# Rounding passes of a feed-forward's weights paired beside a group's sums, and keys and queries set two slots apart

## The chip, the cores and the metric

The kernel runs on one core of a Trainium2 chip. The metric is the device time of one launch in microseconds; the number given is the median of several runs. TensorE, VectorE (DVE), ScalarE (ACT), GpSimd (POOL) and SyncE (SP) each work through a queue of their own, in its order; an instruction that needs another engine's result, or a buffer that another engine still reads, waits at the head of its queue, and all that stands behind it waits too.

## What is computed

Two layers over `x` of shape (4, 512, 256), each a cross-attention on a context and a feed-forward, both behind a layernorm and a gate. Attention has 16 heads of width 16. Shortened from the reference:

```python
x = x + tanh(g_xattn[0]) * L0_xattn(layernorm(x), ctx, ctx)   # scores + time bias, softmax
x = x + tanh(g_ffn[0]) * L0_ffn(layernorm(x))
x = x + tanh(g_xattn[1]) * L1_xattn(layernorm(x), ctx, ctx)
x = x + tanh(g_ffn[1]) * L1_ffn(layernorm(x))                 # routed to one of four experts
```

The first feed-forward uses ternary weights. This is what the rounding passes compute:

```python
def _quantize(W):
    gamma = jnp.mean(jnp.abs(W))
    return jnp.clip(jnp.round(W / (gamma + EPS)), -1.0, 1.0)
h = relu(einsum('bsd,fd->bsf', x, _quantize(W1)) + b1)
out = einsum('bsf,df->bsd', h, _quantize(W2)) + b2
```

Rounding and clipping together mean +1 where a weight is above half of (gamma + EPS), -1 where it is below minus that half, and 0 between.

## The kernel before

**Groups and slots.** Attention is cut into groups of four heads: two layers, four batch elements and four groups each make 32 groups, and each group has four *slots*, one for each 128 positions of the keys. The loop over `u` (L1250) walks 128 such slots. In each, `scores` (L498) puts on TensorE four products of 512 columns for the maxima of a slot six ahead (`pm`) and four for the softmax weights of this slot (`psc`). VectorE reduces each `pm` to a maximum (L512), ScalarE turns each `psc` into exponentials (L527), and in layer 0 GpSimd multiplies a 128 x 256 part of these by a decay (L530, called a *map* below). The eight products take the eight PSUM banks in turn, so the next product on TensorE needs the bank of the slot's first `pm`, which its maximum has to empty.

**Fixed jobs of a slot.** Every fourth slot (`u % 4 == 0`) starts with `weighted` (L555), the *sums* of the group just finished: 16 matmuls of 512 columns, which the trace shows as 32 rows. Where `u % 4 == 2`, `shifted` (L569, L571) and, in the first batch element and in layer 1, `divided` (L606 to L616) follow. For the other batch elements of layer 0 `divided_blocks` (L586 to L596) stands in slots with `u % 4 == 0`.

**The planner.** All other work lies in chains: lists of steps with a cost for TensorE and a gap in slots to the step before. `chain(steps, start, end, *after)` counts due slots back from `end`. In each slot the planner (`slot`) takes, among the chains that are ready, the step that is due first, as long as the slot's cost stays within `SLOT` = 3.1 or the step has no cost or is due. The order in which jobs are called is the order in each engine's queue; no other scheduler moves anything on TensorE, VectorE, ScalarE and GpSimd.

**The steps that the change touches.** `quantize` returns, for each of the two weights (`w1` and `w2`, each 128 x 2048 numbers in place): `totals`, two halves of the sum of absolute values on ScalarE; `total` (L283) and `limits` (L287 on TensorE, L290 to L292 on VectorE), which make the two thresholds `thr`; then for each of four parts of 512 columns `under(i)` (L299), a GpSimd pass that marks what is below the lower threshold, and `over(i)` (L306), a VectorE pass that reads the weights and that mark, and writes the rounded weights. In before these eight passes form one chain with at least one slot between neighbours, `under(i)` ahead of `over(i-1)`; `w1`'s chain starts in slot 4, `w2`'s in slot 17, behind it.

`project(layer, b, tt)` gives two steps: `keys` (a product at L455, then two VectorE passes at L465 in layer 0) and `queries` (a product at L455, then, for layer 0 and the first two batch elements, two ScalarE passes at L485). For the second batch element of layer 0 they stand, both in one slot, in slots 5 and 13.

Around them: `output_bias` (L265 to L269) in slot 6; the layernorm statistics of the third batch element (L329, L330) in slots 18 and 19, with its small GpSimd steps (`more_stats`, L334 to L347) in slot 19 and its rows on ScalarE (L360) in slot 20; `output_biases` of the first feed-forward (L631, a GpSimd pass over 128 x 1024) in slot 19; two `product` steps with the weight `wo` (L383, L388) in slots 21 and 22. `w1` is first read in slot 27 (L668), `w2` in slot 35.

The slots of the passes in before, and of keys and queries of the second batch element:

| step | slots before |
|---|---|
| `limits` of w1; w2 | 6; 18 |
| `under(0..3)` of w1 | 7, 8, 10, 12 |
| `over(0..3)` of w1 | 9, 11, 13, 15 |
| `under(0..3)` of w2 | 19, 20, 22, 24 |
| `over(0..3)` of w2 | 21, 23, 25, 27 |
| keys and queries, first half of the heads | 5, 5 |
| keys and queries, second half | 13, 13 |

Of the kernel before, what the change touches and what calls it, by code (L numbers as in the profile page):

```python
# [41 lines left out]
LEAD = 6  # L42
# [9 lines left out]
def flamingo_kernel(ctx: ExitStack, tc: tile.TileContext, t: dict, out: bass.AP):  # L52
# [11 lines left out]
    def bank_psum(name):  # L64
        return ps.tile([P, 512], F32, tag="bank", name=name)
# [43 lines left out]
    def weight_place(name):  # L109
        return wts.tile([P, NC * FF + NF], F32, tag="wff", name=name)  # L110

    w1f, w2f = (weight_place(name)[:, 0 : NC * FF] for name in ("w1q", "w2q"))
# [159 lines left out]
    def quantize(flat, name):  # L272

        thr = sml.tile([P, 2], F32, tag="qthr", name=f"qthr_{name}")
        part = sml.tile([P, 4], F32, tag="qpart", name=f"qpart_{name}")

        def totals(i0):
            for i in (i0, i0 + 1):
                dump = wts.tile([P, 512], F32, tag="h", name=f"abs_{name}{i}", bufs=8)
                nc.scalar.activation(dump, flat[:, ts(i, 512)], AF.Abs, accum_out=part[:, i : i + 1])  # L280

        def total():
            nc.vector.tensor_reduce(part[:, 0:1], part, AX.X, ALU.add)  # L283

        def limits():
            tot = bank_psum(f"qtot_{name}")
            nc.tensor.matmul(tot[:, 0:1], lhsT=ones, rhs=part[:, 0:1], start=True, stop=True)  # L287

            mean = sml.tile([P, 1], F32, tag="qmean", name=f"qmean_{name}")
            nc.vector.tensor_scalar(mean, tot[:, 0:1], 1.0 / (D * FF), 1e-5, ALU.mult, ALU.add)  # L290
            nc.vector.tensor_scalar(thr[:, 0:1], mean, 0.5, None, ALU.mult)
            nc.vector.tensor_scalar(thr[:, 1:2], mean, -0.5, None, ALU.mult)  # L292

        negs = {}

        def under(i):
            def run():
                negs[i] = wts.tile([P, 512], F32, tag="h", name=f"neg_{name}{i}", bufs=8)
                nc.gpsimd.tensor_scalar(negs[i], flat[:, ts(i, 512)], thr[:, 1:2], None, ALU.is_lt)  # L299

            return run

        def over(i):
            def run():
                w = flat[:, ts(i, 512)]
                nc.vector.scalar_tensor_tensor(w, w, thr[:, 0:1], negs[i], ALU.is_gt, ALU.subtract)  # L306

            return run

        return [  # L310
            (totals, 0, 0), (total, 0, 1), (limits, 0.2, 1),
            (under(0), 0, 1), *((f, 0, 1) for i in range(1, 4) for f in (under(i), over(i - 1))),
            (over(3), 0, 2),
        ]


    def layernorm(src, dst, eps, name, eng=None, meanwhile=None):
# [130 lines left out]
    def project(layer, b, tt):  # L448

        nm = f"{layer}_{b}{tt}"  # L450

        def product(w, src, name):
            pp = bank_psum(f"{name}{nm}")
            for c in range(NC):
                nc.tensor.matmul(  # L455
                    pp, lhsT=attn_w[layer][w][:, c, ts(tt, P)], rhs=src[:, c, :],
                    start=(c == 0), stop=(c == NC - 1),
                )
            return pp

        def key_half(pk, e):
            k = act.tile([P, S], F32, tag="k", name=f"k{nm}{e}", bufs=5)
            h = half[:, e : e + 1]
            if layer == 0:
                nc.vector.scalar_tensor_tensor(k, pk, h, kext[tt, e], ALU.mult, ALU.add)  # L465
            elif e == 0:
                nc.scalar.activation(k, pk, AF.Relu, bias=kone[:, e : e + 1], scale=h)
            else:
                nc.vector.tensor_scalar(k, pk, h, kone[:, e : e + 1], ALU.mult, ALU.max)
            ks[layer, b, tt, e] = k  # L470

        def keys(between=None, halves=range(2)):
            pk = product("wk", cT[b], "pk")
            if between:
                between()
            for e in halves:
                key_half(pk, e)

        def queries():
            pq = product("wq", xTs[layer, b], "pq")  # L480
            for e in range(2):
                q = act.tile([P, S], F32, tag="q", name=f"q{nm}{e}", bufs=4)
                h = half[:, e : e + 1]
                if layer == 0 and (e == 0 or b < 2):
                    nc.scalar.activation(q, pq, AF.Identity, bias=bqk[:, 0, tt, e : e + 1], scale=h)  # L485
                elif layer == 0:
                    nc.vector.tensor_scalar(q, pq, h, bqk[:, 0, tt, e : e + 1], ALU.mult, ALU.add)
                elif e == 0:
                    nc.scalar.activation(q, pq, AF.Relu, scale=h)
                else:  # L490
                    nc.vector.tensor_scalar(q, pq, h, 0.0, ALU.mult, ALU.max)
                qs[layer, b, tt, e] = q

        return [(keys, 1.75, 1), (queries, 1.75, 0)]
# [633 lines left out]
    def chain(steps, start, end, *after):  # L1128
        last = [end] * len(steps)
        for i in range(len(steps) - 2, -1, -1):  # L1130
            last[i] = last[i + 1] - max(steps[i + 1][2], 1 if steps[i][1] and steps[i + 1][1] else 0)
        c = dict(steps=list(zip(steps, last)), ready=start, after=after, done=None)
        chains.append(c)
        return c

    def first_unit(layer, b):
        return 4 * NT * (B * layer + b)
# [3 lines left out]
    for b in range(B):  # L1141
        first, rest = ffn0(b)
# [4 lines left out]
    for layer in range(2):  # L1147
        for b in range(B):
            u0 = first_unit(layer, b)
            lead, values = prepare(layer, b)  # L1150
            if (layer, b) == (0, 1):
                *early, early_rows, turn_1 = (job for job, *_ in lead)
                (early_values, *_), later_values = values
                turned_1 = chain([later_values, (turn_1, 0.9, 1)], 1, 4)
                chain(project(layer, b, 0), 5, u0 - LEAD - 2, turned_1)
            elif u0:
                chain(
                    [*lead, *project(layer, b, 0)], u0 - 14, u0 - LEAD - 2,
                    ffns[b] if layer else None,
                )  # L1160
                chain(values, u0 - 8, u0 + 2)
            chain(project(layer, b, 1), max(u0 - 4, 0), u0)
    (totals1, *_), *quant1 = quantize(w1f, "w1")
    (totals2, *_), *quant2 = quantize(w2f, "w2")
    totals = {0: (totals1, 0), 1: (totals1, 2), 2: (totals2, 0), 3: (totals2, 2)}
    quant = chain(quant1, 4, 17)
    chain(quant2, 17, 33, quant)
    chain([(bias_columns, 0, 0), (output_bias, 0.9, 2)], 4, 14)
    def step(f, *args, cost=0, gap=0):
        return (lambda: f(*args), cost, gap)  # L1170
# [7 lines left out]
    for b in range(B - 1):  # L1178
        u0 = first_unit(1, b + 1)
# [70 lines left out]
    for u in range(-NT, n_units):  # L1250
# [22 lines left out]
        if u in totals:  # L1273
            job, i = totals[u]
# [83 lines left out]
    first = LISTS[2][1]  # L1358
# [131 lines left out]
```

## Time and profile before

| what | value |
|---|---|
| median of three runs | 844.43 us (844.37 to 845.02) |
| the profiled execution's own time | 841.69 us |
| its span, first to last instruction | 839.6 us |
| granted TensorE clock, mean | 0.993 |
| slots 5 to 16, start of slot 5 to start of slot 17 on TensorE | 54.32 to 107.24 us |
| sums in slots 8, 12, 16 on TensorE | from 69.41 to 72.98, 85.4 to 88.96, 103.67 to 107.24 us |
| DMA queues, largest share of the span | 9.3% |

A row of instructions in order of time gives the start (us from the span's start), the length from the first start to the last end, engine, line, operation, what is written and read, shapes, how many followed each other, and in brackets how long the engine was idle ahead of it and what ended that. A row of groups gives, behind the bar, the busy time, the mean of one in ns, and the idle time ahead with its releasers. `PEld` is TensorE's weight load, which runs beside matmuls and shows best when TensorE had to wait. The engines' shares of busy time are means over stages with different limits, so what a slot costs has to be read from that slot.

### The profile page before, as it was taken

Reading aid. Unit: us, or ns where it says so; the run is one execution under the profiler, and the core shown is the slowest. Engines: PE = TensorE matmul, PEld = TensorE weight load, DVE = VectorE, ACT = ScalarE, POOL = GpSimd, SP = SyncE. Lnnn points to the kernel's source line nnn. Section 1 sums busy time; section 2 is a strip of 40 time slices with the busy share of each in tenths; the row PEclk is TensorE's granted clock in tenths of the full one; section 3 lists DMA queues with packets and bytes.
Section 4 is the critical chain, followed back from the end, with each engine's and each line's share of the span. In section 5 each row is a group of like instructions: output and inputs, shape, how many; then the busy total and the mean of one; then the engine's idle time right before and its main releaser. Section 6 shows DMA issues by size and latency. Waiting matters only on the chain. (4 is left out here: it accounts for less than half of the span.)

```text
span 839.6 us, 13573 instructions
## 1 busy us (share of the span) xinstructions
PE 809.5 (96%) x5220; PEld 452.3 (54%) x5220; DVE 568.7 (68%) x1272; ACT 422.1 (50%) x884; POOL 270.3 (32%) x439
## 2 busy tenths in 40 slices
PE   6999999999999999999999999999999999997995
PEld 3444344535464345544474444554445546896994
DVE  6868868766857676567746777448688663886443
ACT  2575555653645453455526475336655667332341
POOL 5636445524233253321101030002103422544522
PEclk9999999999999999999999999999999999998998
DMA  9200000000001000000000000000104331736620
GB/s 313 72 1 1 1 1 1 1 1 1 1 1 39 1 1 1 1 27 1 1 1 26 1 24 28 1 1 1 52 1 152 126 106 59 284 119 218 241 78 31
DMA packets 17712, 42.27 MB, mean 50 GB/s; under 512 B 2033, under 2 KB 12017, under 8 KB 15217
## 3 DMA queue, kind: packets, MB, share of 16 engines
q0 software_dynamic: 5104, 27.34, 9.3%
q1 hardware_dynamic: 12128, 13.54, 4.8%
q8 instruction: 41, 0.67, 0.3%
q10 hardware_dynamic: 416, 0.54, 0.2%
q14 instruction: 23, 0.18, 0.1%
HBM read 35.13 MB, written 6.29 MB: 49 GB/s over the span
## 5 line engine op out<-in xcount | busy, mean ns | idle before, releaser
L512 DVE TENSOR_REDUCE m<-pm 128x1 f32<-128x512 f32 x512 | 316.8, 682 | 107.2 <-PE psc L498 104.8
L527 ACT ACTIVATE p<-psc 128x512 f32<-128x512 f32 x512 | 267.1, 602 | 151.4 <-PE psc L498 148.9
L498 PE MATMUL psc<-q,k 32*128 32x512 f32 x1024 | 278.3, 622 | 0.2 <-DVE h L676 0.2
L498 PE MATMUL pm<-k,q 32*128 32x512 f32 x1024 | 262.2, 615 | 1.5 <-ACT q L485 0.9
L530 POOL TENSOR_TENSOR p<-p,dec 128x256 f32<-128x256 f32 x128 | 93.6, 735 | 177.1 <-ACT p L527 177.1
L498 PEld LDWEIGHTS pm<-k,q 32*128 32x128 f32 x1024 | 92.7, 184 | 83.8 <-issue 49.8
L498 PEld LDWEIGHTS psc<-q,k 32*128 32x128 f32 x1024 | 106.2, 183 | 51.6 <-issue 25.5
L555 PE MATMUL po<-p,v 128*32 128x512 f32 x1024 | 116.5, 595 | 1.9 <-DVE m L512 1.9
L555 PEld LDWEIGHTS po<-p,v 128*32 128x32 f32 x1024 | 31.7, 109 | 81.8 <-issue 60.8
L1090 PE MATMUL pg<-xs,wg 128*128 128x128 f32 x608 | 71.6, 276 | 0.4 <-DVE m L512 0.4
L1090 PEld LDWEIGHTS pg<-xs,wg 128*128 128x128 f32 x608 | 69.8, 192 | 3.8 <-DVE m L512 1.4
L623 POOL TENSOR_TENSOR x<-x,o 128x256 f32<-128x256 f32 x14 | 10.2, 728 | 174.4 <-DVE o L616 131.7
L1116 ACT ACTIVATE ha<-pg,wg 128x128 f32<-128x128 f32 x120 | 34.2, 368 | 53.6 <-PE pg L1090 53.6
L668 PE MATMUL ph<-xTf,w1q 128*128 128x512 f32 x128 | 60.0, 605 | 0.0
L1285 PE MATMUL pyf<-wo,ha 128*128 128x256 f32 x256 | 58.6, 384 | 0.0
L561 ACT COPY oT<-po 128x512 f32<-128x512 f32 x32 | 18.7, 584 | 77.1 <-PE po L555 77.1
L383 PE MATMUL py_f<-w2q,h 128*128 128x256 f32 x256 | 57.2, 381 | 0.0
L383 PEld LDWEIGHTS py_f<-w2q,h 128*128 128x128 f32 x256 | 48.0, 190 | 9.4 <-DVE m L512 3.0
L1285 PEld LDWEIGHTS pyf<-wo,ha 128*128 128x128 f32 x256 | 48.4, 194 | 6.2
L455 PE MATMUL pk<-cT,wk 128*128 128x512 f32 x68 | 35.3, 644 | 7.2 <-DMA cT<-in_ctxT_dram 7.2
L668 PEld LDWEIGHTS ph<-xTf,w1q 128*128 128x128 f32 x128 | 22.6, 189 | 30.4 <-issue 18.2
L388 DVE SCALAR_TENSOR_TENSOR x<-py_f,tg,x 128x512 f32<-128x512 f32 x8 | 6.0, 751 | 42.8 <-PE py_f L383 42.8
(256 smaller groups left out, 814.6 us busy)
## 6 DMA issues: line engine op xcount, KB each, us to landing
x<-in_x_dram SPq DMA_DIRECT2D x4, 512.0 KB, 8.8
rows_d<-xn_f SPq DMA_DIRECT2D x4, 512.0 KB, 3.0
rows_d<-x SPq DMA_DIRECT2D x4, 512.0 KB, 3.6
cT<-in_ctxT_dram SPq DMA_DIRECT2D x3, 512.0 KB, 9.6
w1q<-in_w_dram SPq DMA_DIRECT2D x1, 1024.0 KB, 8.9
w2q<-in_w_dram SPq DMA_DIRECT2D x1, 1024.0 KB, 11.2
wo<-in_wo_dram SPq DMA_DIRECT2D x2, 512.0 KB, 3.8
rows<-in_rows_dram SPq DMA_DIRECT2D x1, 640.0 KB, 9.1
```

The source lines that it names most:

```text
L383: nc.tensor.matmul(py[:, n, :], lhsT=operand(c, n0 + n), rhs=w[:, c, :], start=(c == 0), stop=(c == chunks - 1),)
L455: nc.tensor.matmul(pp, lhsT=attn_w[layer][w][:, c, ts(tt, P)], rhs=src[:, c, :], start=(c == 0), stop=(c == NC - 1),)
L498: nc.tensor.matmul(out_, lhsT=lhs[r, ts(n, P)], rhs=rhs[r, :], start=True, stop=True)
L512: nc.vector.tensor_reduce(m[:, n, 2 * pair + i, r : r + 1], pm[i], AX.X, ALU.max)
L527: nc.scalar.activation(p[:, i, :], psc[i], AF.Exp, scale=SCALE)
L530: nc.gpsimd.tensor_tensor(d, d, dec.unsqueeze(1).to_broadcast([P, 2, P]), ALU.mult)
L555: nc.tensor.matmul(po[i * HP : (i + 1) * HP, :], lhsT=v_sb[b % 2][0][:, kt, c0 : c0 + HP], rhs=ps_exp[NT * s + kt, i // 2][:, i % 2, :], s ...
L561: nc.scalar.copy(pos[s], po)
L668: nc.tensor.matmul(ph, lhsT=w1q[:, c, ts(f, P)], rhs=st["xT"][:, c, :], start=(c == 0), stop=(c == NC - 1),)
L1090: nc.tensor.matmul(ph[:, f, :], lhsT=w[:, c, ts(f2 * NF // 2 + f, P)], rhs=xs[j][:, c, :], start=(c == 0), stop=(c == NC - 1),)
L1116: nc.scalar.activation(ha[:, f, :], (ha if src is None else src)[:, f, :], AF.Gelu, bias=biases[j][:, fa : fa + 1],)
L1285: nc.tensor.matmul(py, lhsT=hs[j, f // 4][:, f % 4, :], rhs=wo1[f // 4][:, f % 4, :], start=(f == 0), stop=(f == NF - 1),)
```

## The change

`quantize` no longer returns one list of nine steps with gaps of one slot but `totals` and three parts: the thresholds with the first two `under` passes; the first two `over` passes with the last two `under` passes; the last two `over` passes. Each part becomes a chain of its own with a first slot: 4, 8 and 12 for `w1`, and 17, 20 and 28 for `w2`. Slots 8, 12, 20 and 28 are slots with sums. In them the two `over` steps, which have no cost, follow at once on each other and are called behind `weighted`.

For the second batch element of layer 0 `queries` gets a gap of two slots to `keys`, in both halves.

The resulting order, read from the built program:

| step | slots after |
|---|---|
| `limits` of w1; w2 | 5 (behind keys); 18 |
| `under(0..3)` of w1 | 5, 6, 8, 9 |
| `over(0..3)` of w1 | 8, 8, 12, 12 |
| `under(0..3)` of w2 | 18, 19, 20, 21 |
| `over(0..3)` of w2 | 20, 20, 28, 28 |
| keys and queries, first half of the heads | 5, 7 |
| keys and queries, second half | 13, 15 |

In slot 19 `under(1)` of w2 stands on GpSimd behind `more_stats` and `output_biases`. All jobs from slot 29 on keep their places, and so do all DMAs.

```diff
-        return [
-            (totals, 0, 0), (total, 0, 1), (limits, 0.2, 1),
-            (under(0), 0, 1), *((f, 0, 1) for i in range(1, 4) for f in (under(i), over(i - 1))),
-            (over(3), 0, 2),
-        ]
+        return (
+            totals, [(total, 0, 0), (limits, 0.2, 1), (under(0), 0, 0), (under(1), 0, 1)],
+            [(over(0), 0, 0), (over(1), 0, 0), (under(2), 0, 0), (under(3), 0, 1)],
+            [(over(2), 0, 0), (over(3), 0, 0)],
+        )
...
-                chain(project(layer, b, 0), 5, u0 - LEAD - 2, turned_1)
+                keys_1, (queries_1, cost, _) = project(layer, b, 0)
+                chain([keys_1, (queries_1, cost, 2)], 5, u0 - LEAD - 2, turned_1)
...
-            chain(project(layer, b, 1), max(u0 - 4, 0), u0)
-    (totals1, *_), *quant1 = quantize(w1f, "w1")
-    (totals2, *_), *quant2 = quantize(w2f, "w2")
-    totals = {0: (totals1, 0), 1: (totals1, 2), 2: (totals2, 0), 3: (totals2, 2)}
-    quant = chain(quant1, 4, 17)
-    chain(quant2, 17, 33, quant)
+            keys_2, (queries_2, cost, _) = project(layer, b, 1)
+            apart = 2 if (layer, b) == (0, 1) else 0
+            chain([keys_2, (queries_2, cost, apart)], max(u0 - 4, 0), u0)
+
+    totals = {}
+    for i, (w, name, first, second, third) in enumerate(((w1f, "w1", 4, 8, 12), (w2f, "w2", 17, 20, 28))):
+        sums, *parts = quantize(w, name)
+        totals |= {2 * i: (sums, 0), 2 * i + 1: (sums, 2)}
+        quant = None
+        for part, u in zip(parts, (first, second, third)):
+            quant = chain(part, u, u + 6, quant)
```

## The prediction

> **What bounds the kernel now.** I read the busy page first, then the instructions of slots 4 to 29 in order of time on each engine, because the edit touches nothing else. [...]
>
> ```profile
> PE 809.5 (96%) x5220; PEld 452.3 (54%) x5220; DVE 568.7 (68%) x1272; ACT 422.1 (50%) x884; POOL 270.3 (32%) x439
> L512 DVE TENSOR_REDUCE m<-pm 128x1 f32<-128x512 f32 x512 | 316.8, 682 | 107.2 <-PE psc L498 104.8
> ```
>
> TensorE is busy 96%, yet its matmul ends are modelled, so I look for its waits. VectorE is 68% busy on average but not evenly. Its order of time in slots 9 to 13:
>
> ```profile
> 74.14 2.48 DVE L512 TENSOR_REDUCE m<-pm 128x1 f32<-128x512 f32 x4 [3.46 <-PE psc L498]
> 76.54 1.16 DVE L306 SCALAR_TENSOR_TENSOR w1q<-w1q,qthr_w,neg_w 128x512 f32<-128x512 f32 x1
> 77.62 2.47 DVE L512 TENSOR_REDUCE m<-pm 128x1 f32<-128x512 f32 x4
> ...
> 81.23 2.47 DVE L512 TENSOR_REDUCE m<-pm 128x1 f32<-128x512 f32 x4
> 83.62 1.02 DVE L306 SCALAR_TENSOR_TENSOR w1q<-w1q,qthr_w,neg_w 128x512 f32<-128x512 f32 x1
> 84.57 2.47 DVE L512 TENSOR_REDUCE m<-pm 128x1 f32<-128x512 f32 x4
> ```
>
> From 74.14 to 86.97 VectorE never rests: here it is the bound, and each rounding pass (L306) pushes the next maxima (L512) back by about a whole pass. TensorE follows, as its weight loads show:
>
> ```profile
> 74.89 0.29 PEld L498 LDWEIGHTS pm<-k,q 32*128 32x128 f32 x2 [0.73 <-DVE m L512]
> ```
>
> The scores of slot 10 wait for a bank that the first maximum of slot 9 empties, 0.75 us after 74.14. Yet ahead of 74.14 VectorE sat idle 3.46 us: TensorE ran the 16 x 2 products of a group's sums (L555, 3.57 us). So I call M(u) the start of slot u's maxima and use three measured rules. TensorE's first extra job of slot u starts no earlier than M(u)+0.77 (its bank); one keys, queries or wo product takes 1.8; M(u+1) is the later of TensorE's slot start plus 1.16 (55.48 against 54.32) and VectorE's own end. The steps M to M, slots 5 to 16, of before: 5.56, 4.77, 2.40, 5.93 | 3.48, 3.61, 3.34, 5.55 | 5.56, 3.68, 3.48, 5.55, together 52.91 us.
>
> **Part 1: rounding w1 beside the sums.** The passes leave slots 9, 11, 13, 15 and stand two by two in slots 8 and 12. A slot with nothing extra steps 2.40 us (slot 7). Slot 9 goes 3.48 to 2.40, slot 11 3.34 to 2.40, slot 15 3.48 to 2.40: 1.08 + 0.94 + 1.08 = **-3.10 us**. The pass of slot 13 ran at 94.24 with its maxima only due at 95.68; it is worth nothing. The added pairs: 2 x 1.08 = 2.16 us, in front of idle 3.46 (slot 8) and 3.08 (slot 12), so nothing, with 0.9 to spare. Their inputs (L299, 1.56 us each on GpSimd) now stand in slots 5, 6, 8, 9, well ahead.
>
> **Part 2: keys and queries two slots apart.** TensorE's work is the same; 1.8 us leaves slots 5 and 13 for 7 and 15. Slot 5: the key halves end at M+4.2 (94.32 against 90.12 in slot 13), and the threshold's three small passes (0.42) now follow them: 4.6. Slot 6 loses these: VectorE's 2.40 + 0.68 + 0.25 + 0.42 + 0.41 = 4.2. Slot 7: 0.84 + 1.77 + 1.16 = 3.76. Slot 8: 5.57 plus 0.4, because the last score now waits for the bank that ScalarE's two query passes hold (nearest row: a sums slot after a queries slot, 88, took 5.98 on TensorE, other sums slots 5.57). Sum 18.53, before 18.66. Slots 13 to 16: 4.1, 3.61, 3.77, 5.97 = 17.45; before 18.27, or 17.19 with slot 15's pass already taken off. So the split alone is -0.13 + 0.26 = **+0.1 us**, that is nothing; ends -0.9 (no bank wait in 8 and 16) to +0.9 (double). It fills slots whose slack Part 1 has just taken.
>
> **Part 3: w2 takes the same form.** The first pair moves to slot 20, ahead of the maxima of slot 21. Its second pass needs the `under(1)` of slot 19, which stands on GpSimd behind the layernorm's small steps and the output bias. In before:
>
> ```profile
> 119.31 2.45 DVE L512 TENSOR_REDUCE m<-pm 128x1 f32<-128x512 f32 x4
> 125.00 2.48 DVE L512 TENSOR_REDUCE m<-pm 128x1 f32<-128x512 f32 x4 [3.25 <-PE psc L498]
> ```
>
> ```profile
> 119.48 0.23 POOL L334 TENSOR_SCALAR var_a<-mv_a 128x4 f32<-128x4 f32 x1 [1.20 <-DVE mv_a L330]
> ...
> 122.39 2.37 POOL L631 TENSOR_TENSOR x<-x,rows 128x1024 f32<-128x1024 f32 x1
> 124.75 1.57 POOL L299 TENSOR_SCALAR neg_w<-w2q,qthr_w 128x512 f32<-128x512 f32 x1
> 126.29 1.42 POOL L530 TENSOR_TENSOR p<-p,dec 128x256 f32<-128x256 f32 x2
> ```
>
> The GpSimd row that ends at 126.3 is `under(0)` in before; after, that one runs at 115.9 to 117.5 in slot 18, in idle time (the two maps of slot 19, at 115.83 and 117.56 in before, then end by 118.9, still ahead of 119.48), and `under(1)` takes its place. So the second pass can start at about 126.35, while slot 21's maxima, queued behind it, were due at 125.00. This is a **new wait**: 126.35 + 1.1 = 127.45, 2.45 us late. Who waits for them: the wo product of slot 21 (the bank of the first maximum). Its load in before:
>
> ```profile
> 125.77 1.59 PEld L383 LDWEIGHTS py_wo<-wo,oTT 128*128 128x128 f32 x8 [0.76 <-DVE m L512]
> ```
>
> It becomes 127.45 + 0.77 = 128.2, and slot 22 follows 2.8 us later as before. TensorE has no slack in slots 21 to 23, so **+2.45 us** stays.
>
> Here a rule speaks against the change. The Trainium skill (SBUF — State Buffer, "Who interferes with whom") says that a VectorE operation with two SBUF inputs and a GpSimd operation that reads SBUF hold a shared port pair exclusively: the later one stands still for the whole of the other. The new pass starts just as two maps (1.42 us, back to back) follow on GpSimd. By the rule it takes 1.42 + 0.74 = 2.16, and the loss is 3.5. The rows differ: at 76.54, beside a map begun at 76.43, the pass took 1.16; at 128.54, inside a GpSimd `under` begun at 127.69, it took 0.74. I take 1.1 and keep 2.16 for the range; the other end is 0.74, a loss of 2.1.
>
> The rest of w2: in before the pass of slot 23 (140.25) delayed slot 24's maxima. M(23) to M(25) is 12.30; the same pair of slots one batch later (39, 40) without a pass took 12.01: **-0.3**. The passes of 21, 25 and 27 were covered by products. The second pair, in slot 28, stands behind the transposes of `divided_blocks`, which end at 166.46; slot 29's maxima start at
>
> ```profile
> 167.43 2.48 DVE L512 TENSOR_REDUCE m<-pm 128x1 f32<-128x512 f32 x4 [0.97 <-PE psc L498]
> ```
>
> so 0.97 us of idle covers only part of 2 x 0.7 (no map runs then): **+0.45**, and the keys product behind waits as much. Ends 0 and +0.9. From slot 30 on the order is unchanged and every step shifts alike; no DMA moves.
>
> **Sum.** -3.10 + 0.1 + 2.45 - 0.3 + 0.45 = **-0.4 us**. The profiled execution took 841.69 (span 839.6, 2.1 around it), giving 841.3; the runs' median is 844.43, so I forecast **844.0**. What a measurement of this kernel tells from no change is about 0.2%, 1.7 us.
>
> **Rivals.**
> *The wait in slot 20 is absorbed* (GpSimd reaches `under(1)` sooner, or slots 21 to 23 have slack I don't see). Against it: GpSimd runs without a gap from 119.48 to 130.6. Then the sum is -2.85: **841.6**.
> *The port decides.* If the lock is as complete as the rule says, the pair of slot 8 meets on GpSimd the two maps and the `under(2)` queued behind: 1.42 + 0.74 + 1.57 + 0.74 = 4.5 us against 3.46 of idle, +1.0; slot 20 costs 3.5 instead of 2.45, +1.05. Sum +1.65: **846.1**, slower. It decides as soon as a pair beside the sums lasts over 3.1 to 3.5 us. For it: 1.16 against 0.74; against it: the 0.74 at 128.54.
> *The change doesn't do what it says*: the planner could have left jobs where they were. The built order shows all moves as told, so this has next to no weight.
>
> **How the numbers follow.** Forecast 0.60, with its own range 842.7 to 845.4 (split and slot 28 together at their ends, 1.35 either way; the pass of slot 20 between its ends stays inside). Wait absorbed 0.18; port 0.20; anything else 0.02. To leave out no more than 2 in 10 the range goes to 842.0 to 846.6. Under 842.7 lie the absorbed wait and a tail: 0.23. Over 846.1 lie half of the port case and a tail: 0.18. Between: 0.59.
>
> **What would show it.** Right: in slots 8 and 12 two L306 rows follow the maxima at once and VectorE still idles ahead of slots 9 and 13; slots 9 and 11 step 2.4; slots 7 and 8 together step about 9.7; in slot 20 one L306 row has an idle of some 4 us released by GpSimd's L299, and slot 21's maxima step 8 us after slot 20's instead of 5.69. Wrong: no such idle (absorbed), L306 rows over 1.5 us (port), or steps of slots 8 and 16 above 6.5 (the bank of the queries costs more than I gave it).

## The result

The changed kernel takes **847.4 us** (median of 11 runs, 846.19 to 850.71) against 844.43 for the kernel before (842.71 to 845.38). The ratio is **1.0039**, 95% interval 1.0029 to 1.005: slower, clear of the noise, and outside the forecast range of 842.0 to 846.6. The profiled execution took 847.52 us, its span is 845.4, and the mean granted clock is 0.989 (before 0.993).

The shares of the page hardly move. The busy page of the changed kernel, and its row of the maxima:

```profile
PE 813.3 (96%) x5220; PEld 453.0 (54%) x5220; DVE 570.7 (68%) x1272; ACT 421.9 (50%) x884; POOL 270.9 (32%) x439
L512 DVE TENSOR_REDUCE m<-pm 128x1 f32<-128x512 f32 x512 | 317.0, 682 | 106.1 <-PE psc L498 103.0
```

VectorE has the same work, within 2 us, and stands idle ahead of its maxima for 1.1 us less than before (106.1 against 107.2). Where the time went can be read only slot by slot. The table gives the step from the start of one slot's maxima to the next slot's, taken from the L512 rows of each trace; slots from 2 to 29 that are not listed differ by less than 0.05 us.

| slot | before | predicted | after | second profile of after |
|---|---|---|---|---|
| 5, 6, 7, 8 | 5.56, 4.77, 2.40, 5.93 | 4.6, 4.2, 3.76, 5.97 | 4.43, 3.99, 4.21, 6.23 | same as after |
| 9, 10, 11, 12 | 3.48, 3.61, 3.34, 5.55 | 2.40, 3.61, 2.40, 5.55 | 2.40, 3.61, 2.39, 5.93 | same |
| 13, 14, 15, 16 | 5.56, 3.68, 3.48, 5.55 | 4.1, 3.61, 3.77, 5.97 | 4.12, 3.61, 4.32, 6.23 | same |
| **5 to 16** | **52.91** | **49.94** | **51.47** | **51.47** |
| 20 | 5.70 | 8.15 | **8.69** | 8.70 |
| 21 | 4.73 | unchanged | 4.69 | **6.36** |
| 23, 24 | 6.75, 5.56 | together 0.3 less | 6.08, 5.92 | 6.09, 5.91 |
| 28 | 5.57 | 6.02 | 5.81 | 5.81 |
| **5 to 29** | **118.00** | 117.6 | **119.41** | **121.09** |

From slot 30 to slot 100 the steps of before and after agree. The two losses that matter most are in slots 20 and 21, and the second one is missing from the first profile of the changed kernel.

The pairs beside the sums do what was forecast. VectorE in order of time in slots 7 and 8 of the changed kernel (start, length, ..., and in brackets the idle time ahead and what ended it):

```profile
69.71 2.48 DVE L512 TENSOR_REDUCE m<-pm 128x1 f32<-128x512 f32 x4 [1.73 <-PE psc L498]
72.11 2.39 DVE L306 SCALAR_TENSOR_TENSOR w1q<-w1q,qthr_w,neg_w 128x512 f32<-128x512 f32 x2
75.94 0.69 DVE L512 TENSOR_REDUCE m<-pm 128x1 f32<-128x512 f32 x1 [1.43 <-PE psc L498]
```

The pair takes 2.39 us and VectorE still idles 1.43 us ahead of the next maxima: it costs nothing there. Slot 20 looks different. VectorE, and below it GpSimd, of the changed kernel:

```profile
119.47 2.45 DVE L512 TENSOR_REDUCE m<-pm 128x1 f32<-128x512 f32 x4
121.83 0.74 DVE L306 SCALAR_TENSOR_TENSOR w2q<-w2q,qthr_w,neg_w 128x512 f32<-128x512 f32 x1
127.03 1.20 DVE L306 SCALAR_TENSOR_TENSOR w2q<-w2q,qthr_w,neg_w 128x512 f32<-128x512 f32 x1 [4.45 <-POOL neg_w L299]
128.16 2.47 DVE L512 TENSOR_REDUCE m<-pm 128x1 f32<-128x512 f32 x4
```

```profile
121.92 0.71 POOL L344 TENSOR_TENSOR rstd_a<-rstd_a,fix_a 128x4 f32<-128x4 f32 x1
...
123.07 2.37 POOL L631 TENSOR_TENSOR x<-x,rows 128x1024 f32<-128x1024 f32 x1
125.42 1.58 POOL L299 TENSOR_SCALAR neg_w<-w2q,qthr_w 128x512 f32<-128x512 f32 x1
126.96 1.87 POOL L530 TENSOR_TENSOR p<-p,dec 128x256 f32<-128x256 f32 x2
```

The second pass waits 4.45 us for GpSimd's mark, as forecast, and the maxima stand behind it. TensorE is next in the chain of waits. Its row in slot 21 of the changed kernel:

```profile
128.89 1.99 PE L383 MATMUL py_wo<-wo,oTT 128*128 128x256 f32 x8 [2.89 <-DVE m L512]
```

TensorE itself now stands still for 2.89 us, where in before its matmuls went on almost at once. The forecast followed the wait to here and stopped.

### The profile page after: what moved, and what is told of

Its sections match the earlier page's. It is cut to its first block, busy times and chain, and to the rows that moved or that the text cites. A ratio compares the mean times of both kernels' runs of the same rounds, so it can differ in the third digit from the quotient of the medians.

```text
span 845.4 us, 13571 instructions
## 1 busy us (share of the span) xinstructions
PE 813.3 (96%) x5220; PEld 453.0 (54%) x5220; DVE 570.7 (68%) x1272; ACT 421.9 (50%) x884; POOL 270.9 (32%) x439
## 5 line engine op out<-in xcount | busy, mean ns | idle before, releaser
L512 DVE TENSOR_REDUCE m<-pm 128x1 f32<-128x512 f32 x512 | 317.0, 682 | 106.1 <-PE psc L498 103.0
L498 PE MATMUL psc<-q,k 32*128 32x512 f32 x1024 | 281.2, 624 | 0.2 <-DVE h L676 0.2
```

Of the source, the lines that this page charges most:

```text
L498: nc.tensor.matmul(out_, lhsT=lhs[r, ts(n, P)], rhs=rhs[r, :], start=True, stop=True)
L512: nc.vector.tensor_reduce(m[:, n, 2 * pair + i, r : r + 1], pm[i], AX.X, ALU.max)
```

## The experiments

Theory A, going in: the pairs gain about what was forecast, and the wait in slot 20 and the split give it back. Rival B: a loss that lies outside these slots. Rival C: VectorE's and GpSimd's shared port makes the pairs themselves dear. "Slots" is the time of slots 5 to 29 of the profile; before takes 118.00.

| run | median us | before beside it | ratio, 95% interval | slots, against before |
|---|---|---|---|---|
| w1_pairs_only | 842.17 | 844.40 | 0.9974 [0.9964, 0.9984] | -2.34 |
| w2_pairs_only | 848.73 | 844.40 | 1.0056 [1.0042, 1.007] | +4.57 |
| early_mark | 842.64 | 844.40 | 0.9985 [0.9975, 0.9995] | -1.51 |
| both_pairs_early_mark_together | 840.32 | 844.40 | 0.9955 [0.9941, 0.9969] | -2.42 |
| w2_pairs_busy_tensor | 845.78 | 842.84 | 1.0034 [1.0022, 1.0046] | +2.87 |
| mark_before_bias | 844.26 | 842.84 | 1.0011 [1.0001, 1.002] | +0.71 |
| queries_half_vector | 841.91 | 842.84 | 0.9986 [0.9975, 0.9997] | -1.20 |
| after_again | 845.78 (one run) | 842.84 | none | +3.09 |
| mark_before_bias_in_quarters | 841.31 | 843.40 | 0.9971 [0.9959, 0.9983] | -0.84 |
| split_only | 842.45 | 843.40 | 0.9996 [0.9985, 1.0006] | -0.65 |

### One weight alone: w1_pairs_only and w2_pairs_only

Both undo the split, and one of the weights keeps the old chain of nine steps (`CHAINED` is `('w2',)` in the first and `('w1',)` in the second):

```diff
+    CHAINED = ('w2',)
...
+        if name in CHAINED:
+            return totals, [
+                (total, 0, 0), (limits, 0.2, 1),
+                (under(0), 0, 1), *((f, 0, 1) for i in range(1, 4) for f in (under(i), over(i - 1))),
+                (over(3), 0, 2),
+            ]
...
-                keys_1, (queries_1, cost, _) = project(layer, b, 0)
-                chain([keys_1, (queries_1, cost, 2)], 5, u0 - LEAD - 2, turned_1)
+                chain(project(layer, b, 0), 5, u0 - LEAD - 2, turned_1)
```

> Only w1's passes in pairs (slots 8 and 12); w2 as a chain and keys with queries in one slot, as before. In the profiles of before and after, slots 9 to 12 together step 15.98 and 14.33 us, and slot 15 loses its pass (1.08). Theory A (the pairs are right, the wait in slot 20 and the split eat them): slots 5 to 29 together 2.7 us shorter than before, time 841.7, ratio 0.997. Rival B (any reordering of this stage brings the extra 1.6 us that after shows outside these slots): 1.1 us shorter, ratio 0.999. Rival C (a pair meets the GpSimd port lock): a pair lasts over 3 us, slots 9 and 13 start late, ratio 1.000 or above.

> Only w2's passes in pairs (slots 20 and 28), the rest as before. Theory A: slot 20 steps 8.7 us instead of 5.70 (the second pass waits for GpSimd's mark behind the layernorm steps and the output bias), slots 23 and 24 lose 0.3, slot 28 gains 0.24: +2.9 us, 847.3, ratio 1.0035. Rival B (extra 1.6 us outside): +4.5, ratio 1.0053. Rival D (the wait in slot 20 is absorbed when slots 5 to 16 are as before): slot 20 under 6.5 us, ratio 1.0005 or below.

`w1` in pairs is a gain of 2.34 us in the slots and of 0.26% in the time. Slots 9, 11 and 15 fall to 2.40, 2.39 and 2.40 as forecast, 3.11 us together; slots 12 and 16 grow from 5.55 to 5.93 each and give 0.76 back. The pair of slot 8 takes 2.36 us, and VectorE still idles 1.18 us behind it: C falls for `w1`. The time, 2.2 us shorter by the ratio, leaves no loss outside the slots: B falls too.

`w2` in pairs loses 4.57 us: 3.00 in slot 20 and 1.65 in slot 21, which the changed kernel's own profile had left at 4.69. Theory A had expected 2.9 and misses. The size is the 4.5 that B gave, but the extra loss lies inside slot 21 and not outside the slots. (All lines of this run stand 8 lower in its code, so L520 is the maxima and L391 the `wo` product.) TensorE's `wo` rows, and the granted clock in four windows of 2 us (columns: window, its length, busy time of PE, PEld, DVE, ACT and POOL, clock, DMA share, GB/s):

```profile
129.24 3.68 PE L391 MATMUL py_wo<-wo,oTT 128*128 128x256 f32 x8 [2.89 <-DVE m L520]
```

```profile
126.00:128.00 2.00, 0.35 (x4) 0.00 (x0) 0.62 (x1) 2.00 (x6) 2.00 (x2) 1.00 0.00 0
128.00:130.00 2.00, 0.76 (x2) 0.67 (x3) 2.00 (x4) 0.98 (x3) 2.00 (x3) 0.83 0.00 0
130.00:132.00 2.00, 2.00 (x6) 1.56 (x6) 0.98 (x2) 0.00 (x0) 2.00 (x3) 0.50 0.03 8
132.00:134.00 2.00, 2.00 (x15) 1.55 (x17) 0.75 (x1) 0.61 (x2) 1.65 (x2) 0.81 0.00 0
```

TensorE stood still for 2.89 us, the same as in the changed kernel, but here the clock then drops to 0.50, and eight matmuls that took 1.99 us take 3.68. The same window of the changed kernel's first profile:

```profile
130.00:132.00 2.00, 2.00 (x17) 1.69 (x19) 1.38 (x3) 0.64 (x2) 2.00 (x4) 1.00 0.03 8
```

### The wait taken away: early_mark and both_pairs_early_mark_together

`early_mark` is the changed kernel with both marks of `w2` in slot 18, where GpSimd has time; the other run also undoes the split.

```diff
-            totals, [(total, 0, 0), (limits, 0.2, 1), (under(0), 0, 0), (under(1), 0, 1)],
+            totals, [(total, 0, 0), (limits, 0.2, 1), (under(0), 0, 0), (under(1), 0, 0 if name == "w2" else 1)],
```

> After, with one number changed: the gap ahead of w2's second mark is 0, so that both marks stand in slot 18 on GpSimd, ahead of slot 19's layernorm steps. Theory A: slot 20 falls from 8.69 to about 5.7 us and no idle released by the mark remains; the kernel gains 3.0 us on after; slots 5 to 29 are 1.5 us shorter than before, time 842.9 if nothing differs outside them (ratio 0.998), 844.5 if the 1.6 us outside stays (Rival B, ratio 1.000). Rival C (port lock): the second pass still lasts over 1.5 us. Risk named beforehand: the norm rows of slot 20 on ScalarE come up to 1 us later, which the idle ahead of them (2 us) covers.

> As early_mark, and keys and queries of the second batch element in one slot again. Tells the price of the split. Theory A: the split costs 1.3 us (slots 7, 8, 15, 16 step 4.21, 6.23, 4.32, 6.23 in after), so this one is 1.3 us faster than early_mark and 2.8 us faster than before: 841.6, ratio 0.9967. Rival (the split is worth nothing, as I predicted, +0.1): same as early_mark. Rival B: 1.6 us above these numbers.

Slot 20 is back at 5.70 us and slot 21 at 4.72. Placing one mark a slot earlier, on an engine that is busy 32% of the time, turns the slower kernel into a faster one (0.9985). Without the split it is 0.9955: this version beats both kernels. Slots 5 to 16 take 51.49 us with the split and 50.58 without: in the paired kernel **the split costs 0.91 us**, where the prediction had +0.1 and the expectation of this run 1.3. The two profiled executions lie 1.0 us apart (spans of 842.2 and 841.2), the medians 2.3 us; why the medians show more was not followed.

### Is slot 21 the gap, or something else? w2_pairs_busy_tensor and after_again

```diff
-        for kt in range(NT):
+        again = [(kt, kt == NT - 3) for kt in range(NT - 2)] if s == 4 else []
+        for kt, last in again + [(kt, kt == NT - 1) for kt in range(NT)]:
             for i in range(HG):
...
-                    start=(kt == 0), stop=(kt == NT - 1),
+                    start=(kt == 0), stop=last,
```

> w2 in pairs alone, and in slot 20 TensorE runs the first two of the four key blocks of group 4's weighted sums twice (16 more of the L563 matmuls, some 1.8 us by their row of 3.64 us for 32; the second pass overwrites the first, so the output stays). It fills TensorE's gap ahead of slot 21's scores, which was 2.89 us in w2_pairs_only, to about 1.1 us, and leaves VectorE's wait for GpSimd's mark as it was. Theory (the clock gate answers to the gap): slot 20 still takes about 8.7 us, but the granted clock stays at 1.00 at 128 to 134 us, the eight py_wo matmuls take 2.0 us instead of 3.68, slot 21 takes 4.7 instead of 6.37, slots 5 to 30 take about 120.9 us instead of 122.57; ratio to before about 1.0035 (847.3). Rival (slot 21's loss is not the gap: late work of ScalarE or GpSimd, or a busy-power throttle): slot 21 stays at 6.3 and the ratio at 1.0056 or above, since TensorE has more work and not less.

> The changed kernel once more, unedited, for a second profile. Theory (TensorE's 2.89 us gap ahead of slot 21 trips the clock gate in most executions but not in all): slot 20 takes 8.69 us again, and slot 21 takes either 4.7 us (clock 1.00) or about 6.3 us (clock about 0.5 at 128 to 132 us); slots 5 to 30 are 119.4 or 121.0. Rival (slot 21 is fixed by the program): exactly 4.69 again with no other value in any run of a kernel with this gap.

w2_pairs_busy_tensor is w2_pairs_only with 16 matmuls of slot 20's sums done twice. TensorE gets more to do and the kernel gets faster: 1.0034 instead of 1.0056. Here (L391 and L520 as above) the gap is 1.19 us:

```profile
129.00 1.99 PE L391 MATMUL py_wo<-wo,oTT 128*128 128x256 f32 x8 [1.19 <-DVE m L520]
```

Slot 20 keeps its wait (8.72), the granted clock is 1.00 in each of the four windows, and slot 21 takes 4.69. The second profile of the unedited changed kernel, after_again, shows the drop that the first did not (same columns, windows of 3.41 us):

```profile
125.13:128.54 3.41, 0.99 (x5) 0.89 (x6) 2.85 (x4) 2.16 (x5) 3.41 (x4) 1.00 0.00 0
128.54:131.95 3.41, 3.41 (x13) 2.71 (x11) 1.50 (x3) 0.59 (x1) 3.40 (x4) 0.50 0.02 5
```

So the gap is the cause: of three profiles with a gap of 2.89 us two show half the clock and a slot 21 of 6.36 to 6.37, one shows 1.00 and 4.69, and with the gap filled (one profile) both the drop and its 1.7 us are gone. The intervals of the two ratios, 1.0034 and 1.0056, just overlap. The two results for the slots, +1.41 and +3.09 us, stand beside a measured 0.39%, 3.3 us, which suggests that most executions pay. How many is not shown.

The traces hint at why one of the three escaped. In the two others the clock stands at 0.50 for 3.41 us (128.54 to 131.95 and, in w2_pairs_only, 129.33 to 132.74), and within each trace all changes of the clock lie a whole number of such stretches apart. The stretch ahead of the drop in w2_pairs_only:

```profile
125.92:129.33 3.41, 0.52 (x5) 0.09 (x1) 1.95 (x3) 3.06 (x7) 3.41 (x4) 1.00 0.00 0
```

And the two stretches that share the gap in the changed kernel's first profile, counted from a drop at 28.47 to 31.88 us:

```profile
124.04:127.45 3.41, 1.96 (x20) 0.87 (x16) 0.42 (x1) 3.31 (x7) 3.41 (x3) 1.00 0.00 0
127.45:130.86 3.41, 1.97 (x10) 1.72 (x11) 3.18 (x5) 1.18 (x3) 3.41 (x4) 1.00 0.00 0
```

Where 2.89 and 2.42 us of one stretch lay idle on TensorE, the next stretch ran at 0.50; where the gap fell across a border, some 1.45 us on either side, the clock stayed. This is a reading of three profiles: no run moved the border. It is not the whole rule either, since a drop at 572.59 us in w1_pairs_only follows a stretch in which TensorE was busy for 2.94 us.

### How complete is the shared port? mark_before_bias and mark_before_bias_in_quarters

The changed kernel with `under(1)` of `w2` ahead of the bias addition (L631); the second run also splits that addition for the first batch element.

```diff
-            quant = chain(part, u, u + 6, quant)
+            quant = chain(part, u, 20 if u == 17 else u + 6, quant)
```

```diff
-            nc.gpsimd.tensor_tensor(
-                x[b], x[b], bo0.unsqueeze(1).to_broadcast([P, NT, D]), ALU.add
-            )
+            if b:
...
+            for n in range(NT):
+                nc.gpsimd.tensor_tensor(x[b][:, n, :], x[b][:, n, :], bo0, ALU.add)
```

> The changed kernel with one edit: w2's second mark (under(1), GpSimd L299) is issued before the output bias's 2.37 us addition (L631) instead of behind it. VectorE's second pass then runs beside that addition. By the rows (a pass beside GpSimd work took 1.16 to 1.20 us instead of 0.74): the mark ends near 124.5, the pass near 125.8, slot 20 takes 6.2 to 6.4 us instead of 8.69, TensorE's gap falls to about 0.5 us, no clock drop in slot 21 (step 4.7), slots 5 to 30 take about 117.0; ratio to before 0.999 (843.5). By a full exclusive port (the pass starts only when the 2.37 us addition is over): slot 20 takes about 7.9 to 8.7 us as before the edit and the ratio is 1.002 to 1.004.

> mark_before_bias with one more edit: for the first batch element the output bias (L631) is added in four GpSimd instructions of 128x256 instead of one of 128x1024. In mark_before_bias VectorE's second pass stood beside the undivided addition and took 2.83 us, ending 0.55 us after the addition's end. Theory (GpSimd holds the shared port for one instruction, and VectorE's pass gets in between two): the pass waits for the rest of the first quarter (about 0.65 us of 0.72) and takes about 1.2 us, the second quarter is stretched to about 1.2, slot 20 takes about 6.4 us instead of 8.00, slots 5 to 30 about 117.1 instead of 118.71; ratio to before about 0.999. Rival (a pass stands still for as long as GpSimd has work queued, or the 2.83 us has to do with the length of the data and not of the instruction): the pass takes 2.8 to 3.3 us, slot 20 stays at 8.0 or above, ratio 1.001 or above.

The first is a miss for the reading by rows. Slot 20 takes 8.00 us and not 6.3, as the exclusive port had it; the ratio, 1.0011, is below the 1.002 expected for that case. VectorE, then GpSimd, of mark_before_bias:

```profile
123.39 2.83 DVE L306 SCALAR_TENSOR_TENSOR w2q<-w2q,qthr_w,neg_w 128x512 f32<-128x512 f32 x1 [2.13 <-POOL neg_w L299]
```

```profile
123.32 2.35 POOL L631 TENSOR_TENSOR x<-x,rows 128x1024 f32<-128x1024 f32 x1
125.63 1.86 POOL L530 TENSOR_TENSOR p<-p,dec 128x256 f32<-128x256 f32 x2
```

The addition began 0.07 us before the pass and ends at 125.67. The pass ends at 126.22, **0.55 us later**: it stood still for all of it, and the maps behind the addition took 1.86 instead of 1.42 because the pass then came first. With the addition in quarters:

```profile
123.19 1.21 DVE L306 SCALAR_TENSOR_TENSOR w2q<-w2q,qthr_w,neg_w 128x512 f32<-128x512 f32 x1 [2.13 <-POOL neg_w L299]
```

```profile
123.12 3.24 POOL L637 TENSOR_TENSOR x<-x,rows 128x256 f32<-128x256 f32 x4
```

The first quarter ran from 123.12 to 123.85, and the pass ends at 124.40, again 0.55 us later; the second quarter takes 1.18 us instead of about 0.73. Slot 20 falls to 6.37, and the kernel is faster than before (0.9971). In these rows the lock is complete, and it lasts for one instruction.

### The split: queries_half_vector and split_only

queries_half_vector is early_mark with one more edit; split_only is the kernel before with the change to keys and queries alone.

```diff
-                if layer == 0 and (e == 0 or b < 2):
+                if layer == 0 and (e == 0 or b < 1):
                     nc.scalar.activation(q, pq, AF.Identity, bias=bqk[:, 0, tt, e : e + 1], scale=h)
                 elif layer == 0:
                     nc.vector.tensor_scalar(q, pq, h, bqk[:, 0, tt, e : e + 1], ALU.mult, ALU.add)
```

> The changed kernel with both w2 marks early (early_mark) and one more edit: the second of the two query passes of the second batch element (L485, 0.72 us on ScalarE) goes to VectorE, so that the two passes run side by side. Theory (slots 8 and 16 are 6.23 us because the queries, now two slots behind the keys, come just ahead of the scores that use them, and their two ScalarE passes end late): the scores start about 0.7 us earlier, slots 8 and 16 fall from 6.23 to about 5.6 to 5.95, and the sum of slots 5 to 17 from 51.5 to about 50.7; ratio to before 0.9970 to 0.9978 against early_mark's 0.9985. Rival (the cost of the split is on VectorE or in the keys): the added VectorE passes of 0.75 us each come on top or change nothing, the sum stays at 51.5 to 53, ratio 0.9985 or above.

> The kernel before with the queries of the second batch element two slots behind the keys and nothing else; the rounding passes stay where they were. Theory (the split costs 0.9 us in the changed kernel only because it fills slots 7 and 15, which the pairs had emptied or left empty; against a kernel whose slot 15 holds a rounding pass anyway it costs little): slots 5 to 9 take about 18.9 us (before 18.66), slots 13 to 17 between 17.9 and 18.6 (before 18.28), slots 5 to 17 between 52.7 and 53.5 (before 52.91), ratio 0.9995 to 1.0008. Rival (the split itself costs 0.9 us or more, through the bank that the query passes hold): slots 5 to 17 at 53.8 or above, ratio 1.001 or above.

queries_half_vector: slots 8 and 16 fall from 6.23 to 5.92, as the theory had it, but slots 7 and 15 grow by 0.48 and 0.49, as the rival had it, and slots 5 to 16 take 51.82 us instead of 51.49. VectorE's query pass stands ahead of its maxima, and it does not run beside ScalarE's but behind it:

```profile
68.15 0.81 DVE L487 TENSOR_SCALAR q<-pq,cols,bqk 128x512 f32<-128x512 f32 x1 [1.48 <-ACT q L485]
```

So this run could not show what an earlier free bank would bring. Its ratio, 0.9986, is that of early_mark.

split_only misses the expected range on the good side: 52.27 us in slots 5 to 16 against 52.91. The rounding passes did not stay where they were. With the queries out of slot 5 the planner puts `limits` there, and the whole chain of `w1` moves up a slot: its passes stand in slots 8, 10, 12 and 14. Two of the four then lie beside sums, free of charge, and slots 9 to 12 fall from 15.98 to 14.99. The slots that hold keys and queries, 5 to 8 and 13 to 16, cost 0.19 and 0.15 more. In time it is nothing (0.9996). So this is not the clean test that it was meant to be: the split's own price, 0.34 us, is covered by the 0.98 that the moved chain gains. It does speak against the rival, which wanted 53.8 us or more.

## Why the prediction was wrong

| term | forecast | measured | by |
|---|---|---|---|
| `w1` pairs | -3.10 | -2.34 | w1_pairs_only |
| split | +0.1 | +0.91 | early_mark against both_pairs_early_mark_together |
| wait in slot 20 | +2.45 | +2.99 | steps of after |
| slots 23, 24 | -0.3 | -0.30 | steps of after |
| slots 28, 29 | +0.45 | +0.20 | steps of after |
| clock in slot 21 | not in the sum | +1.64 in two of three profiles | after_again, w2_pairs_only, w2_pairs_busy_tensor |
| sum | -0.4 | +3.1 | after_again: +3.09 |

**The step that failed** is the last sentence of Part 3's main argument, "TensorE has no slack in slots 21 to 23, so +2.45 us stays". The wait was followed from GpSimd to VectorE to TensorE, and its length was carried through unchanged. That holds for the length alone. What happens to TensorE's speed when it stands still was put at nothing, without a reason. Its matmuls after the gap ran at half the granted clock in two of three profiles, and slot 21 took 1.64 us more. The Trainium skill (TensorE: Matmul & The Clock Gate, Part 1) says that the gate halves the rate after an idle window of about 3.4 us and that the window runs freely, without starting anew with the kernel; its list of rules (Why this matters for your kernels) asks for no gaps above about 3 us. The traces agree on the length, 3.41 us, but a window that was not wholly idle was enough: TensorE had been busy for 0.52 and 0.99 us of it, in a gap of 2.89 us by the matmul rows or 3.71 to 3.72 counted from the last weight load. A gap of 2.19 us left the clock alone (mark_before_bias, one profile), but there the gap lies across a border of two windows, 0.86 and 1.33 us, so this sets no limit for the length. Before the change the same load waited 0.76 us, so this was a price the change brought in. Without it the time would have lain about 1.6 us lower in the executions that paid: inside the range, though still above the forecast, since the terms below are together some 1.9 us off.

**The `w1` pairs** were right in mechanism and mis-sized by 0.76 us. The slots that lose a pass fall just as forecast. The rule "TensorE's first extra job of slot u starts no earlier than M(u)+0.77" was then used as if the job started at that moment. It holds while VectorE is late. After a slot with nothing extra TensorE is the one that is late: its own eight products end about 1.2 us after M. In slots 12 and 16 the sums, which started 0.82 us after M in before, now start 1.20 us after it, 0.38 us later each.

**The split** was mis-sized for the same reason, at the same rule. In slot 7 the maxima start at 64.16 and the query product at 65.30 (after_again), 1.14 us later and not 0.77; slots 7 and 15 measured 4.21 and 4.32 against 3.76 and 3.77. The wait for the bank that the query passes hold is real, too, and has the size given to it, 0.44 us against 0.4. The weight load of the last scores ahead of slot 8's sums, in the changed kernel:

```profile
70.16 0.29 PEld L498 LDWEIGHTS psc<-q,k 32*128 32x128 f32 x2 [0.44 <-ACT q L485]
```

Slots 8 and 16 measured 6.23 against 5.97: their sums start 1.50 us after M, and 1.20 without the split, where these slots take 5.93 (both_pairs_early_mark_together). Against this slots 5 and 6 came out 0.17 and 0.21 lower than forecast. What is left is that the split puts a product into slots 7 and 15, which after the pairs hold nothing else and in which TensorE, and not VectorE, sets the end.

**The wait in slot 20** was right in place, sender and chain, and 0.54 us too small. About 0.5 of that is the step L344, which took 0.71 us instead of 0.20: it began 0.09 us after VectorE's first pass and ended 0.06 after it, and everything behind it on GpSimd moved. The pass itself took 1.20 us against 1.1. Slots 28 and 29 came out 0.25 us better than forecast; this was not followed.

**The rule and the row.** The forecast set 2.16 us by the skill's rule of the exclusive port (SBUF — State Buffer, "Who interferes with whom") against 1.16 from a row, and took the row. Both readings were off. The row was an instance of the rule: in before the map that began at 76.43 ended at 77.15, and the pass ended at 77.70, 0.55 us later, as in the two experiments above. And the rule was read too widely: in these traces the port is held for one instruction, so of two maps back to back the pass waits for one, 0.66 + 0.55 = 1.2 us, which is what slot 20 shows. Taken from the row alone, the pass beside L631 would have cost 1.2 us; it cost 2.83.

**The rivals.** "The port decides" needed pairs of over 3.1 to 3.5 us; they took 2.39 in slot 8 and 1.88 in slot 12. The lock is there, but the pair met one map and one mark, and not all that was queued. "The wait is absorbed" fell with the row of 4.45 us. The forecast's own signs came out as told, but for the steps of 7 and 8 together, 10.44 instead of 9.7: that was the mark of the mis-sized rule.

## What to carry over

When work is moved into another engine's idle time, check that its inputs are there as well: the slot had room on VectorE, but its input stood behind 2.4 us of other work on GpSimd, and placing that input one slot earlier turned +0.39% into -0.15%. A wait that reaches TensorE has a second price beside its length, since a gap of 2.89 us halved the clock behind it in two of three profiles; a stall that ends on TensorE should be costed with and without that. And when slack is taken out of a slot, the next engine's own end becomes the limit, so a rule that was measured where one engine is late has to be measured again where it is not.

## What the runs showed of the hardware

- In these traces the shared port of VectorE and GpSimd works by turns of one instruction. A two-input pass on VectorE that meets a running GpSimd TENSOR_TENSOR ends 0.55 us after that instruction, whether it lasts 0.72 us (the maps) or 2.35 us (the bias). The other way round a GpSimd instruction that begins during a pass waits for it: a map took 1.22 instead of 0.72, a step of 128x4 0.71 instead of 0.20. The mark (L299, TENSOR_SCALAR, one input) is milder, but not free: a pass that began 0.85 us into one took its 0.74 us without any delay (128.54 in before), a pass that began 0.49 us into one took 1.17 (73.33 in the changed kernel), and a mark that began with a pass or during one took 2.00 to 2.10 instead of 1.56.
- The clock also drops elsewhere, in some executions. Near the start of a launch the first profile of the changed kernel has 0.62 and 0.53 at 28 to 32 us and starts slot 2 at 44.96 us; the second has 1.00 there and starts it at 43.62. early_mark and both_pairs_early_mark_together show the same early drop, the profile of before does not. Both of them and w1_pairs_only also drop to 0.50 for 3.41 us near 573 us, and take 1.05 us more in slots 30 to 100 than the others. In slots 113 to 115 the first profile of the changed kernel takes 1.7 us more than before or the second, at a clock of 1.00, for a reason that stays open. A profile's total can therefore differ by 1 to 3 us for no reason of the change, which is why the readings above rest on steps of slots and on ratios of several runs. Differences of this size also remain between ratios and steps: 0.9955 (3.8 us) beside -2.42 us for both_pairs_early_mark_together, and 0.9971 (2.4 us) beside -0.84 us for mark_before_bias_in_quarters. This was not followed further.
